# Seven block products in place of eight, in the experts' gate and up products and in the attention's output products of a two-layer block; one reordering of the up-projections' blocks

## The chip, the cores and the metric

The kernel runs on one core of a Trainium2 chip, as one program. The metric is the device time of one execution in microseconds. A "unit" below is one head of one batch row in the attention; a "tile" of the experts is one block of 128 gate columns and the 128 up columns that belong to it.

## The reference, cut to what matters

Two layers act on a residual stream of 4 x 512 rows of 512 values, all in float32. Layer 0 adds a test-time-training attention (a recurrence over 32 mini-batches of 16 tokens) and a gated feed-forward of 1408. Layer 1 adds a latent attention with 16 heads, here on sequences of 512, and four experts, each of which sees every fourth token. The change is in layer 1:

```python
xn = _layernorm(x)
# attention: latents c_kv (128) and c_q (384), 16 heads of 128, rotated first 64 dimensions
ctx = jnp.einsum('bhqk,bkhd->bqhd', softmax(q @ k / sqrt(D)), v).reshape(b, s, H * D)
attn = ctx @ W_O + b_O
# experts: token g*4 + e goes to expert e
gu = jnp.einsum('bgeh,ehd->bged', x4, gate_up_proj)
gate, up = (gu[..., :I], gu[..., I:])
inter = jax.nn.silu(gate) * up                     # I = 512
out = jnp.einsum('bgei,eih->bgeh', inter, down_proj)
x = x + attn + out.reshape(B, N, H)
```

## The kernel before, in words

The kernel has three stages, one after the other, with tile pools of their own.

**Layer 0** (0 to 967 us). The recurrence over mini-batches and the rest of the layer share the engines: `fill()` takes pieces of the feed-forward, of the projections and of the finishing of chunks from a generator (`between`, `take`) into the gaps of the recurrence. The stage goes through 8 chunks of 256 rows. In each, `gate_up` (L447 on) makes 11 blocks of the feed-forward: it loads `wg` and `wu` by SP's DMA queue (L454), multiplies 128x128 weights into 256 columns and puts both results into the two halves of one PSUM bank, `pf`; ACT applies Silu to the gate half (L458), VectorE multiplies (L459). `kv<-rows` (L290) and `z`, `zb` (L437, L439) are trips through DRAM on which the recurrence and the finishing of a chunk wait; `latents` writes the latents of layer 1 to DRAM (`lat_d`).

**Experts** (967 to 1145 us). `hidden(e)` makes, for each of 4 blocks of 128 gate columns, eight matmuls of 512 tokens: four into bank `pg` over the 512 input values and four into `pu` (`product`, L916 to L920). ACT applies Silu to `pg` (L946) and VectorE multiplies by `pu` into `inter` (L947). `returned(e)` multiplies `inter` by the down weights and adds into `y` (L961, L968). Two buffers of each bank are in turn. Beside them, `fold` prepares the weights of the first four heads of the attention.

**`fold`** (L821 on) is run once for each quarter of the heads. Of five matrices (`W_UK`, three blocks of `W_UQ`, `W_UV`) it loads four 128x128 blocks each (`raw`), as 16 DMAs of 16 KB in runs of 128 bytes (L856), so that VectorE's transposition within 32x32 squares (L846) gives the whole transpose. Matmuls then fold the rotation's weights (`pw`, L841) and the output weights (`pvo`, L865) in; `vo` holds, for each of 4 heads, 128 latent values by 512 outputs.

**Attention** (1145 to 2069 us). There are 64 units, 4 heads in each of 16 groups (4 quarters of the heads by 4 batch rows). Iteration i of the loop issues, in this order: queries and keys of unit i (`pk` L1047, `pq` L1055, rotations on VectorE and POOL L1030 to L1040), scores and softmax of unit i - 1 (`sc` L1065, maximum L1067, exponential L1070, scaling L1075, VectorE's transposition in squares L1094, then 16 DMAs that turn the blocks, `prT<-tt` L1125), one quarter of the output of a finished group (`po` L1146, added into `y` by VectorE at L1155), and the context of unit i - 3 (`pc` L1133, copied to `ctxT` by ACT at L1135). From the second step of a unit on, a step of `fold` follows. In the last two iterations two quarters of an output are made. `pin` keeps this order on PE, ACT and VectorE; POOL and the DMA queues are ordered by the scheduler. `pk`, `pq`, `po`, `pc`, `pw` and `pvo` take the four banks of one pool in turn, the scores another four. The last group's output is made in parts, as its heads become ready, with the last head's probabilities turned by PE.

The queries' latents `cq` of all four batch rows lie in SBUF throughout the attention, loaded once.

Of the kernel before, what the change touches and what calls it, by code (L numbers as in the profile page):

```python
# [12 lines left out]
F32 = mybir.dt.float32  # L13
# [5 lines left out]
P = 128  # L19
# [36 lines left out]
def trunk_kernel(ctx: ExitStack, tc: tile.TileContext, a: dict, out: bass.AP):  # L56
# [16 lines left out]
    lat_d = dram.tile([1 + QC // P, P, B, NCHUNK, CT], F32, tag="lat_d", name="lat_d")  # L73
    bo = const.tile([P, HS], F32, tag="bo", name="bo")
    eps_ttt = const.tile([P, 1], F32, tag="eps_ttt", name="eps_ttt")
    nc.vector.memset(eps_ttt, TTT_EPS)
# [12 lines left out]
    with ExitStack() as px:  # L89
# [9 lines left out]
        def mm(out, lhsT, rhs, start=True, stop=True):  # L99
            nc.tensor.matmul(out, lhsT=lhsT, rhs=rhs, start=start, stop=stop, skip_group_check=True)  # L100
# [347 lines left out]
        def gate_up(ch, i):  # L448
            if i == 0:
                hid[ch] = wk.tile([P, NI, CW], F32, tag="hid", name=f"hid_{ch}", bufs=1)  # L450
            pf = ps_ff.tile([P, 2, CW], F32, tag="pf", name=f"pf_{ch}_{i}")
            for j, nm in enumerate(("wg", "wu")):
                w = wk.tile([P, NC, P], F32, tag=nm, name=f"{nm}_{ch}_{i}")
                nc.sync.dma_start(out=w, in_=a[nm][i])  # L454
                for c in range(NC):
                    mm(pf[:, j, :], w[:, c, :], xTs[ch][:, c, :], c == 0, c == NC - 1)
            sg = wk.tile([P, CW], F32, tag="sg", name=f"sg_{ch}_{i}")
            nc.scalar.activation(sg, pf[:, 0, :], AF.Silu, scale=gs[:, i : i + 1])  # L458
            nc.vector.scalar_tensor_tensor(  # L459
                hid[ch][:, i, :], pf[:, 1, :], us[:, i : i + 1], sg, ALU.mult, ALU.mult  # L460
            )
            yield 3.43
# [330 lines left out]
    ckv = lat.tile([P, B, L], F32, tag="ckv", name="ckv")  # L793
    cq = lat.tile([P, QC // P, B, L], F32, tag="cq", name="cq")

# [18 lines left out]
    ups = ["uk"] + [f"uq{i}" for i in range(QC // P)]  # L814

    def group_tiles(pool, hg):
        w = {nm: pool.tile([P, HPG, D], F32, tag=nm, name=f"{nm}_{hg}", bufs=1) for nm in ups}
        w["vo"] = pool.tile([P, HPG, HS], F32, tag="vo", name=f"vo_{hg}", bufs=1)
        return w

    def fold(w, hg, wk, psum, bufs, pin=lambda ins: ins, ahead=1, rows=nc.sync):  # L821

        c = slice(hg * HPG * D, (hg + 1) * HPG * D)
        srcs = [a["W_UK"][:, c]] + [a["W_UQ"][i * P : (i + 1) * P, c] for i in range(QC // P)]
        for nm, src in zip(ups, srcs):
            nc.sync.dma_start(out=w[nm][:, :, :RD], in_=src.rearrange("p (h d) -> p h d", h=HPG)[:, :, :RD])
        srcs.append(a["W_UV"][:, c])
        raws, turned, ows = {}, {}, {}
# [4 lines left out]

        n = len(srcs)
        for i in range(n + 1 + ahead):
            k = i - ahead - 1
            if 0 <= k < n - 1:
                wt, wr, to = turned.pop(k), wqr if k else wkr, w[ups[k]]
                pw = psum(f"pw_{hg}_{i}").rearrange("p (h d) -> p h d", h=HPG)[:, :, :RD]
                for h in range(HPG):  # L840
                    pin(nc.tensor.matmul(pw[:, h, :], lhsT=wt[:, h, :], rhs=wr, start=True, stop=True))  # L841
                pin(nc.scalar.copy(to[:, :, RD:], pw))
            if 0 <= i - ahead < n:
                t = turned[i - ahead] = wk.tile([P, HPG, P], F32, tag="wt", name=f"wt_{hg}_{i - ahead}", bufs=bufs)
                pin(
                    nc.vector.transpose(  # L846
                        out=t.rearrange("p h c -> p (h c)"), in_=raws.pop(i - ahead).rearrange("p h c -> p (h c)")
                    )
                )
            if i < n:  # L850

                raw = raws[i] = wk.tile([P, HPG, P], F32, tag="raw", name=f"raw_{hg}_{i}", bufs=bufs)
                view = srcs[i].rearrange("(cq r) (h dq d) -> dq r h cq d", r=32, h=HPG, dq=4)
                for dq, r in enumerate(quarters):
                    for h in range(HPG):
                        nc.sync.dma_start(  # L856
                            out=raw[r, h].rearrange("r (cq d) -> r cq d", cq=4), in_=view[dq, :, h]
                        )
            if i - n - ahead + 1 >= 0:
                output_rows(i - n - ahead + 1)  # L860
            yield
# [19 lines left out]
    with ExitStack() as px:  # L881
# [33 lines left out]

        def product(e, ps, w, col):  # L916
            for c in range(NC):
                nc.tensor.matmul(  # L918
                    ps, lhsT=w[:, c, col : col + P], rhs=xe[:, :, c, e, :], start=(c == 0), stop=(c == NC - 1)
                )  # L920

        def by_chunk(ap):

            return ap.rearrange("p (k b j) -> p k b j", k=NCHUNK, b=B)

# [8 lines left out]
        def hidden(e):  # L934

            gu = ws.pop(e)
            inter = inters[e] = wk.tile([P, EI // P, B * P], F32, tag="inter", name=f"inter_{e}")
            for i in range(EI // P):
                if e > 1:
                    next(first, None)  # L940
                pg = ps_gu.tile([P, B * P], F32, tag="pg", name=f"epg_{e}_{i}")
                product(e, pg, gu, i * P)
                pu = ps_gu.tile([P, B * P], F32, tag="pu", name=f"epu_{e}_{i}")
                product(e, pu, gu, EI + i * P)
                sg = wk.tile([P, B * P], F32, tag="sg", name=f"esg_{e}_{i}")
                nc.scalar.activation(sg, pg, AF.Silu)  # L946
                nc.vector.tensor_mul(  # L947
                    by_batch(inter[:, i].rearrange("p (b j) -> p b j", b=B)), by_chunk(pu), by_chunk(sg)
                )
            if e + 2 < E:  # L950
                ws[e + 2] = gates(e + 2)

        def returned(e):
# [4 lines left out]
            for b in range(B):  # L958
# [9 lines left out]
                nc.vector.tensor_add(y[b][:, e, :], po, y[b][:, e, :])  # L968

        for e in range(E):  # L970
            if e == 1:
                nc.sync.dma_start(out=wqr, in_=a["W_QR"])
                nc.sync.dma_start(out=wkr, in_=a["W_KR"])
                buv16 = wk.tile([H, D], F32, tag="buv16", name="buv16", bufs=1)
                nc.sync.dma_start(out=buv16, in_=a["b_UV"].rearrange("(h d) -> h d", d=D))
                w0 = group_tiles(lat, 0)
                first = fold(w0, 0, wk, lambda nm: psp.tile([P, 512], F32, tag="pa", name=nm), 1)
                nc.sync.dma_start(out=buk, in_=a["b_UK"])
# [6 lines left out]
                nc.sync.dma_start(out=ckv, in_=lat_d[0].rearrange("p b k x -> p b (k x)"))  # L985
                for i in range(QC // P):
                    nc.sync.dma_start(out=cq[:, i], in_=lat_d[1 + i].rearrange("p b k x -> p b (k x)"))
            hidden(e)
# [27 lines left out]
    with ExitStack() as px:  # L1016
        wk = px.enter_context(tc.tile_pool(name="e_wk", bufs=2, reuse_waits="tile"))
        ps_pj = px.enter_context(tc.tile_pool(name="e_pspj", bufs=4, space=PSUM))
        ps_sc = px.enter_context(tc.tile_pool(name="e_pssc", bufs=4, space=PSUM))
# [22 lines left out]
        def queries_keys(hg, b, h, w):  # L1042
# [10 lines left out]
            for i in range(nq):  # L1053
                pin(
                    nc.tensor.matmul(  # L1055
                        pq, lhsT=w[f"uq{i}"][:, h, :], rhs=cq[:, i, b, :], start=(i == 0), stop=(i == nq - 1)
                    )
                )
# [71 lines left out]
        def context(prT, b, ctxT, h, nm, pool=ps_pj, tag="pj"):  # L1130
# [8 lines left out]
            )  # L1139

        def project_out(hg, b, e, w, ctxT, heads, po):
            if heads[0] == 0:
                po[e] = ps_pj.tile([P, HS], F32, tag="pj", name=f"po_{hg}_{b}_{e}")
            for h in heads:
# [18 lines left out]
        ws, cs, qk, probs = {}, {}, {}, {}  # L1163
        folds, outs = iter(()), []
        ws[0] = w0
        for i in range(nu + 1):
            if i < nu:
                hg, b, h = units[i]
                if h == 0:
                    if b == 1 and hg + 1 < NHG:  # L1170
# [10 lines left out]
                        )  # L1181
                        next(folds)
                    cs[hg, b] = wk.tile([P, HPG, L], F32, tag="ctxT", name=f"ctxT_{hg}_{b}")
                qk[i] = queries_keys(hg, b, h, ws[hg])
# [4 lines left out]
            for _ in range(1 if i < nu - 1 else 2):  # L1189
                if outs:  # L1190
                    outs.pop(0)()
            if i >= 3:
                hg, b, h = units[i - 3]
                context(probs.pop(i - 3), b, cs[hg, b], h, f"{i - 3}")
                if h == HPG - 1:
                    outs += [
                        (lambda hg=hg, b=b, e=e: project_out(hg, b, e, ws[hg], cs[hg, b], range(HPG), {}))
                        for e in range(E)
                    ]
            if i % HPG != 0:  # L1200
# [115 lines left out]
```

## Time and profile before

| what | value |
|---|---|
| runs | median 2072.76 us of 3 (2068.73 to 2076.26) |
| the profiled execution | 2071.4 us, of which the span from the first to the last instruction is 2069.5 |
| granted TensorE clock | 0.994 |
| `epg` and `epu` matmuls (L918) | 256 instructions, 58.4 and 57.5 us busy |
| `po` matmuls (L1146) | 512 instructions, 230.0 us busy |
| DMAs `raw` (L856) | 320 of 16 KB |
| DMA engines | mean 124 GB/s; q1 43.0% of 16 engines' span |

A row of the groups reads: line, engine, operation, result<-operands by the program's names, shape, count, busy time, mean time of one, and the idle time of the engine before it with what ended it. In the chain and the timeline the first number is the start in us from the span's beginning, the second the length, "x16" the number of instructions merged; in brackets stands the idle time before. SPq is the queue in which SP issues DMAs. A line of the waits gives who waited for whom, the total, how often, and the longest.

### The profile page before, as it was taken

How to read it: one execution, taken by the hardware profiler on the slowest of the kernel's cores; microseconds unless marked ns; L12 is line 12 of the kernel's file. 1: busy time of each engine (PE TensorE's matmuls, PEld its weight loads, DVE VectorE, ACT ScalarE, POOL GpSimd, SP SyncE). 2: the span in 40 equal slices, each digit the busy share in tenths (PEclk: the TensorE clock that was granted, in tenths of full speed). 3: DMA queues.
4: the chain of work that ended last, by engine and by line, in shares of the span. 5: the costliest groups of instructions: out<-in, count | busy, mean ns of one | idle time of the engine just before them, and what ended most of it. 6: DMA issues, size and time to landing. Idle time of an engine off the chain costs nothing.

```text
span 2069.5 us, 29404 instructions
## 1 busy us (share of the span) xinstructions
PE 2008.5 (97%) x9934; PEld 1144.4 (55%) x9934; DVE 1206.6 (58%) x2518; ACT 846.8 (41%) x1701; POOL 494.6 (24%) x559
## 2 busy tenths in 40 slices
PE   8999999899999999999999899999999999999999
PEld 6777676757676767645444344444444444444444
DVE  5446666474747575743121676666666666666662
ACT  2334343333434434312001464555555554555552
POOL 5233333233332323320000211121111111242110
PEclk9999999999999999999999999999999999999999
DMA  6546463545454747564721233443333333423332
GB/s 192 158 135 199 119 203 105 179 138 169 136 167 115 202 140 198 160 217 156 250 61 48 62 87 80 100 96 77 77 91 98 83 78 80 100 70 77 96 96 74
DMA packets 335730, 257.20 MB, mean 124 GB/s; under 512 B 107100, under 2 KB 264989, under 8 KB 334557
## 3 DMA queue, kind: packets, MB, share of 16 engines
q1 hardware_dynamic: 320592, 240.74, 43.0%
q0 software_dynamic: 3488, 9.27, 1.3%
q10 hardware_dynamic: 11500, 5.32, 0.9%
q8 instruction: 80, 1.31, 0.3%
q14 instruction: 70, 0.57, 0.1%
HBM read 159.50 MB, written 29.62 MB: 91 GB/s over the span
## 4 chain that ended last, share of the span: by engine, by line
PE 86%; DVE 7%; DMA 3%; ACT 2%; SPq 2%; issue 1%; POOL 0%; ACTq 0%; DVEq 0%; POOLq 0%
PE pj L100 13%; PE pf L100 12%; PE pc L1133 10%; PE po L1146 10%; PE sc L1065 10%; PE pq L1055 7%; PE pd L100 6%; PE epg L918 3%; PE epo L961 3%; PE epu L918 3%; PE pk L1047 3%; PE pz L100 2%; PE pso L100 1%; SPq L1125 1%; PE wacc L100 1%
## 5 line engine op out<-in xcount | busy, mean ns | idle before, releaser
L1070 ACT ACTIVATE prob<-sc,mx 128x512 f32<-128x512 f32 x256 | 174.5, 684 | 173.6 <-DVE mx L1067 169.6
L1133 PE MATMUL pc<-prT,lv 128*128 128x512 f32 x496 | 226.3, 599 | 8.8 <-issue 4.1
L1065 PE MATMUL sc<-kT,qT 96*128 96x512 f32 x512 | 230.9, 593 | 1.8 <-ACT prob L1070 1.5
L1146 PE MATMUL po<-vo,ctxT 128*128 128x512 f32 x512 | 230.0, 592 | 0.7 <-ACT ctxT L1135 0.7
L1040 POOL TENSOR_TENSOR kT<-t_k,t_k 32x512 f32<-32x512 f32 x64 | 80.7, 1261 | 562.4 <-PE pq L1055 454.8
L1094 DVE STREAM_TRANSPOSE tt<-prob 128x512 f32<-128x512 f32 x252 | 172.8, 705 | 71.5 <-ACT prob L1075 45.1
L100 PE MATMUL pf<-xT,wg 128*128 128x256 f32 x704 | 174.2, 390 | 13.1 <-DVE hid L459 6.8
L1075 ACT ACTIVATE prob<-prob,sm 128x512 f32<-128x512 f32 x256 | 176.5, 714 | 0.0
L1055 PE MATMUL pq<-cq,uq 128*128 128x512 f32 x384 | 175.2, 592 | 0.0
L1067 DVE TENSOR_REDUCE mx<-sc 128x1 f32<-128x512 f32 x256 | 168.3, 678 | 5.8 <-PE sc L1065 3.8
L100 PE MATMUL pf<-xT,wu 128*128 128x256 f32 x704 | 167.7, 381 | 0.0
L1133 PEld LDWEIGHTS pc<-prT,lv 128*128 128x128 f32 x496 | 94.8, 192 | 131.0 <-issue 125.0
L1065 PEld LDWEIGHTS sc<-kT,qT 96*128 96x128 f32 x512 | 96.7, 190 | 125.8 <-issue 120.3
L100 PE MATMUL pd<-wd,hid 128*128 128x512 f32 x352 | 165.6, 600 | 0.6 <-DMA wd<-in_wd 0.5
L1146 PEld LDWEIGHTS po<-vo,ctxT 128*128 128x128 f32 x512 | 96.9, 190 | 123.4 <-issue 118.2
L100 PEld LDWEIGHTS pf<-xT,wg 128*128 128x128 f32 x704 | 132.9, 193 | 40.7 <-DVE hid L459 8.6
L100 PEld LDWEIGHTS pf<-xT,wu 128*128 128x128 f32 x704 | 134.4, 191 | 18.9 <-DMA wu<-in_wu 0.3
L1055 PEld LDWEIGHTS pq<-cq,uq 128*128 128x128 f32 x384 | 73.0, 190 | 91.8 <-issue 90.2
L459 DVE SCALAR_TENSOR_TENSOR hid<-pf,us,sg 128x256 f32<-128x256 f32 x88 | 41.7, 475 | 134.7 <-ACT sg L458 133.7
L1030 DVE SCALAR_TENSOR_TENSOR t_k<-pk,b_UK,trig_k 32x512 f32<-32x512 f32 x64 | 47.9, 748 | 113.0 <-ACT kT L1048 110.9
L297 POOL TENSOR_SCALAR sk<-k,m 128x256 f32<-128x256 f32 x64 | 61.3, 971 | 192.1 <-PE pz L100 172.6
L404 POOL TENSOR_SCALAR gh<-grad,m 128x256 f32<-128x256 f32 x64 | 62.6, 988 | 153.8 <-DVE grad L373 146.2
(251 smaller groups left out, 2994.7 us busy)
## 6 DMA issues: line engine op xcount, KB each, us to landing
prT<-tt SPq DMA_DIRECT2D x1008, 64.0 KB, 2.0
wd<-in_wd SPq DMA_DIRECT2D x176, 256.0 KB, 3.0
wg<-in_wg SPq DMA_DIRECT2D x88, 256.0 KB, 2.8
wu<-in_wu SPq DMA_DIRECT2D x88, 256.0 KB, 3.4
rows<-rows SPq DMA_DIRECT2D x128, 66.0 KB, 2.2
kv<-rows SPq DMA_DIRECT2D x32, 264.0 KB, 4.9
gu<-in_gu SPq DMA_DIRECT2D x3, 2048.0 KB, 7.8
xt<-in_x SPq DMA_DIRECT2D x32, 128.0 KB, 2.9
```

What stands on the lines that cost most here:

```text
L100: nc.tensor.matmul(out, lhsT=lhsT, rhs=rhs, start=start, stop=stop, skip_group_check=True)
L404: nc.gpsimd.tensor_scalar_mul(gh[:, :, h, :], g, m2[:, h : h + 1])
L918: nc.tensor.matmul(ps, lhsT=w[:, c, col : col + P], rhs=xe[:, :, c, e, :], start=(c == 0), stop=(c == NC - 1))
L1040: nc.gpsimd.tensor_sub(t[RD:mid, :], t1[RD:mid, :], t2[RD:mid, :])
L1055: nc.tensor.matmul(pq, lhsT=w[f"uq{i}"][:, h, :], rhs=cq[:, i, b, :], start=(i == 0), stop=(i == nq - 1))
L1065: pin(nc.tensor.matmul(ps, lhsT=qT[:KQ, i * P : (i + 1) * P], rhs=kT[:KQ, :], start=True, stop=True))
L1067: pin(nc.vector.tensor_reduce(mx, ps, AX.X, ALU.max, negate=True))
L1070: pin(nc.scalar.activation(pr, ps, AF.Exp, bias=mx, scale=1.0, accum_out=sm))
L1075: pin(nc.scalar.mul(pr, pr, sm))
L1094: nc.vector.transpose(out=tt[:, :, :, i, :], in_=pr.rearrange("p (kb e j) -> p kb e j", e=2, j=K))
L1133: pin(nc.tensor.matmul(pc, lhsT=lv[:, b, k, :], rhs=prT[:, k, :], start=(k == 0), stop=(k == E - 1)))
L1146: nc.tensor.matmul(po[e], lhsT=ctxT[:, h, e * P : (e + 1) * P], rhs=w["vo"][:, h, :], start=(h == 0), stop=(h == HPG - 1),)
```

## The change

Both places now multiply a 2 x 2 arrangement of blocks by seven block products and fifteen sums (Winograd's form of Strassen's method), with the sums of the right-hand operand made once. The sum that is needed three times is built up in one half of a PSUM bank (`x`), and read out after each of its steps.

- *Experts.* Of a tile, rows of the left matrix are gate and up columns, its columns the two halves of the 512 input values; the right matrix is the tokens, in two halves of 256. `left_sums` (VectorE, four sums of 128x256, one of them in place in the weights) is issued one tile ahead; `right_sums` (four sums of 128x512) once for an expert. A block product is two matmuls of 256 columns. ACT copies `x` and `pu` out four times a tile (`c1`, `c2`, `c3`, `c5`, one buffer each); VectorE makes three additions and two multiplies in place of one multiply.
- *Attention.* Four heads' contexts of a group (a 512 x 512 matrix) by `vo`. The generator `outputs` makes one block product in its first step and two in each of three more, a step to a unit; a block product is four matmuls of 256 columns. POOL makes the sums (`left_operands` for a group, `right_operands` for a quarter of the heads). VectorE adds each result into `y` where it belongs: 8 additions of 128x512 for a group in place of 4. The last group keeps `project_out`. One of the projections' four banks becomes the bank of `x`.
- *Reordering once.* 80 DMAs copy the up-projections' blocks from DRAM to DRAM during layer 0 (`blocks_d`, one after each of the first ten blocks of `gate_up` in each chunk), 64 KB each in runs of 128 bytes; `fold` then loads four blocks with one DMA in place of 16.
- *Room in SBUF.* The queries' latents are loaded for each group (three DMAs of 256 KB, one group ahead, two buffers), and `wt` in `fold` has one buffer. One of the two latent buffers serves the experts for the four copies.

The diff, cut to its core:

```diff
+    blocks_d = dram.tile([QC // P + 2, P, H, P], F32, tag="blocks_d", name="blocks_d")
+    up_srcs = [a["W_UK"]] + [a["W_UQ"][i * P : (i + 1) * P] for i in range(QC // P)] + [a["W_UV"]]
+    def reordered():
+        for k, src in enumerate(up_srcs):
+            view = src.rearrange("(cq r) (h dq d) -> cq dq r h d", r=32, dq=4, d=32)
+            for cq in range(4):
+                for dq in range(4):
+                    nc.sync.dma_start(
+                        out=blocks_d[k, 32 * dq : 32 * dq + 32, :, 32 * cq : 32 * cq + 32], in_=view[cq, dq]
+                    )
+                    yield
...
+            if i < 10:
+                next(copies, None)
...
-    cq = lat.tile([P, QC // P, B, L], F32, tag="cq", name="cq")
+    s_ops = lat.tile([P, 3, 2, L // 2], F32, tag="s_ops", name="s_ops")
+    t_ops = lat.tile([P, 4, 2, HS // 2], F32, tag="t_ops", name="t_ops")
...
-                view = srcs[i].rearrange("(cq r) (h dq d) -> dq r h cq d", r=32, h=HPG, dq=4)
-                for dq, r in enumerate(quarters):
-                    for h in range(HPG):
-                        nc.sync.dma_start(
-                            out=raw[r, h].rearrange("r (cq d) -> r cq d", cq=4), in_=view[dq, :, h]
-                        )
+                nc.sync.dma_start(out=raw, in_=blocks_d[i][:, heads, :])
...
+        def left_sums(gu, i):
+            s1, s2, s4 = (s_ops[:, n, :, i % 2 * P : (i % 2 + 1) * P] for n in range(3))
+            nc.vector.tensor_add(s1, a21, a22)
+            nc.vector.tensor_sub(s2, s1, a11)
+            nc.vector.tensor_sub(a21, a11, a21)
+            nc.vector.tensor_sub(s4, a12, s2)
...
-                product(e, pg, gu, i * P)
-                product(e, pu, gu, EI + i * P)
-                sg = wk.tile([P, B * P], F32, tag="sg", name=f"esg_{e}_{i}")
-                nc.scalar.activation(sg, pg, AF.Silu)
+                pg = ps_gu.tile([P, 2, half], F32, tag="pg", name=f"epg_{e}_{i}")
+                pu = ps_gu.tile([P, half], F32, tag="pu", name=f"epu_{e}_{i}")
+                x = pg[:, 0]
+                block_product(x, o["a11"], tokens(e, 0, 0), True)
+                block_product(pg[:, 1], o["a12"], tokens(e, 1, 0))
+                nc.scalar.copy(c1, x)
+                block_product(x, o["s2"], t_ops[:, 1])
+                nc.scalar.copy(c2, x)
+                block_product(pu, o["s1"], t_ops[:, 0], True)
+                nc.scalar.copy(c5, pu)
+                block_product(x, o["s3"], t_ops[:, 2])
+                nc.scalar.copy(c3, x)
+                block_product(pu, o["s4"], tokens(e, 1, 1))
+                block_product(x, o["a22"], t_ops[:, 3])
+                g = wk.tile([P, 2, half], F32, tag="sg", name=f"esg_{e}_{i}")
+                nc.vector.tensor_add(g[:, 0], pg[:, 1], c1)
+                nc.vector.tensor_add(g[:, 1], pu, c2)
+                nc.scalar.activation(g, g, AF.Silu)
+                nc.vector.tensor_add(c5, c5, c3)
+                for h, up in enumerate((x, c5)):
+                    nc.vector.tensor_mul(to[:, k], by_chunk(up), by_chunk(g[:, h]))
...
-        ps_pj = px.enter_context(tc.tile_pool(name="e_pspj", bufs=4, space=PSUM))
+        ps_pj = px.enter_context(tc.tile_pool(name="e_pspj", bufs=3, space=PSUM))
+        ps_x = px.enter_context(tc.tile_pool(name="e_psx", bufs=1, space=PSUM))
...
+        def block_product(ps, a, w, start=True):
+            for k in range(2):
+                for q in range(2):
+                    pin(nc.tensor.matmul(ps[:, q, :], lhsT=a[:, k, q * P : (q + 1) * P], rhs=w[:, k, :], ...))
...
+            x = bank(ps_x, "px", "px")
+            block_product(x, left_blocks(c)["a11"], r["b11"])
+            add(x, 0, 0)
+            o = left_operands(c)
+            yield
+            p2 = bank(ps_pj, "pj", "p2")
+            block_product(p2, o["a12"], r["b21"])
+            block_product(x, o["s2"], r["t2"], False)
+            add(p2, 0, 0)
+            add(x, 0, 1)
+            yield
+            p5 = bank(ps_pj, "pj", "p5")
+            block_product(p5, o["s1"], r["t1"])
+            block_product(x, o["s3"], r["t3"], False)
+            add(p5, 0, 1)
+            add(p5, 1, 1)
+            add(x, 1, 1)
+            yield
+            p3 = bank(ps_pj, "pj", "p3")
+            block_product(p3, o["s4"], r["b22"])
+            block_product(x, o["a22"], r["t4"], False)
+            add(p3, 0, 1)
+            add(x, 1, 0)
...
             for _ in range(1 if i < nu - 1 else 2):
-                if outs:
-                    outs.pop(0)()
+                next(outs, None)
```

`add` is a pinned `tensor_add` on VectorE into a quarter of `y[b]`; `left_operands` and `right_operands` are four `nc.gpsimd` additions or subtractions each, by the same scheme as `left_sums` and `right_sums`.

## The prediction

> **What bounds the kernel now.** I read the busy times first, then the chain that ended last, then the waits and the timeline of each stage.
>
> ```profile
> span 2069.5 us, 29404 instructions
> PE 2008.5 (97%) x9934; PEld 1144.4 (55%) x9934; DVE 1206.6 (58%) x2518; ACT 846.8 (41%) x1701; POOL 494.6 (24%) x559
> PE 86%; DVE 7%; DMA 3%; ACT 2%; SPq 2%; issue 1%; POOL 0%; ACTq 0%; DVEq 0%; POOLq 0%
> ```
>
> TensorE is busy for 97% of the span and is 86% of the chain: time goes only if matmul time goes. By stages PE is busy 922.1 of 967.0 us (layer 0), 177.8 of 178.0 (967 to 1145, experts) and 908.6 of 924.5 (attention). So both places of the change are bound by PE, and the question is what half-width products cost. Two pieces of the chain:
>
> ```profile
> 506.40 3.65 PE pf L100 x16
> 516.03 3.45 PE pf L100 x16
> ...
> 1185.70 3.44 PE sc L1065 x8
> ```
>
> Sixteen instructions of 256 columns take 3.45 us undisturbed (215.6 ns each), eight of 512 columns 3.44 (430 ns). Each f32 matmul is two instructions, and every one has its own weight load (190 ns), which fits under 215 ns. So half-width products run at full rate, and seven in place of eight save an eighth. (The means of 390 and 592 ns in the groups are latencies.)
>
> **The experts' gate and up products.** For each of 16 tiles, 8 matmuls of 512 columns (16 instructions x 0.430 = 6.88 us) become 14 of 256 (28 x 0.2156 = 6.04): 0.84 saved, 13.5 us in all. What can give it back is the hand-over, since one half bank accumulates three running sums, each copied by ACT before PE goes on.
>
> ```profile
> 828.63 1.89 PE L100 MATMUL pf<-xT,wu 128*128 128x256 f32 x8
> ...
> 830.55 0.47 ACT L458 ACTIVATE sg<-pf,gs 128x256 f32<-128x256 f32 x1 [3.73 <-PE pf L100]
> ```
>
> The gate half was written before 828.63, yet its Silu starts at 830.55, 0.2 us after the last matmul into the other half (issued until 830.35): a reader waits for the whole bank. The rule behind it is in the Trainium skill, "PSUM — Partial Sum Buffer", section "PSUM bank collisions raise a hardware error": two engines must not touch one bank at once. It speaks against packing x and the second half into one bank; without it the loop below would be some 0.9 us shorter and cost nothing, by it 4 us.
>
> ```profile
> 1455.77 0.37 ACT L842 COPY uk<-pw 128x256 f32<-128x256 f32 x1 [0.25 <-PE pw L841]
> ```
>
> - The copy of a sum: 0.2 until ACT starts, 0.37 for a 128x256 copy, 0.05 back, together 0.62. The cover is one block product (0.86) less the prefetched weight load (0.215): 0.645. It just fits: I take 0; if the cover goes, 0.2 a hand-over.
> - The closed loop of a tile: c5 is one buffer, so its next copy waits for the last multiply. From the end of a tile's last product: 0.2, add 0.42 (L523, 128x256), hand-over 0.05, Silu 0.60 (L946), 0.05, two multiplies 2 x 0.42, 0.05, copy 0.37, 0.05 = 2.6; then four block products, 3.45, and a weight load of 0.19 not hidden: 6.25 against 6.04. Cost 0.25 x 16 = 4 us. Bounds: 0 (where `pw`, `pvo` or `epo` matmuls stand between) and 0.8 a tile (all four hand-overs late), 13.
> - VectorE: per tile 4 left sums, 3 adds and 2 multiplies of 256 elements, 9 x 0.42 = 3.8 of 6.0 us, and four sums of 512 an expert (4 x 0.69). It was nearly idle (30.6 busy of 178), so this is hidden, except at the start: VectorE ends layer 0's last latent at 971.0, the PE at 970.0. In the changed program 8 left sums (3.4) and t1 (0.7) follow, so s1·t1 can start at 975.1; PE has four block products ready (3.45) and waits from 973.4 on: 1.7 to 1.9 us. The table load before the first Silu (1.28) pushes the second tile's copies: 1.1.
>
> Sum for the experts: -13.5 + 4 + 1.9 + 1.1 = **-6.5 us** (bounds -13.5 and +1).
>
> **The attention's output products.** For 15 of 16 groups of four heads, 32 instructions x 0.430 = 13.76 become 56 x 0.2156 = 12.07: 1.69 x 15 = 25.3 us. The last group keeps the old form. Here the running sum is handed over a whole unit (one head, 13.7 us) later, so the adds are off the path, but the pool for projections has 3 banks in place of 4. One unit as it is:
>
> ```profile
> 1459.06 3.60 PE L1065 MATMUL sc<-kT,qT 96*128 96x512 f32 x8
> ...
> 1462.50 3.60 PE L1146 MATMUL po<-vo,ctxT 128*128 128x512 f32 x8
> ...
> 1465.93 3.60 PE L1133 MATMUL pc<-prT,lv 128*128 128x512 f32 x8
> ...
> 1468.48 0.65 DVE L1155 TENSOR_TENSOR y<-po,y 128x512 f32<-128x512 f32 x1
> ...
> 1470.22 2.74 PE L1055 MATMUL pq<-cq,uq 128*128 128x512 f32 x6
> ```
>
> VectorE adds an output 9.4 us after the scores begin, behind the four transposes of the softmax, as its order is fixed. `pq` of the next unit now takes the bank of this output (three back in the rotation): released at 10.07, or at 10.72 in the step with two adds of p5; its weights load at 10.74. It just fits: 0 to 0.1 us a group, 0.5 in all; if VectorE fell behind by 1 us, 1 us in 45 units. Four more adds a group (4 x 0.65) fall where VectorE waits 2.1 us for ACT anyway. POOL gets 4 sums a group (L1205: 1.27 each, 5.1 us), 4 more once for each quarter of the heads; it idles 9.9 us a unit, and rotations pushed back 5 us are needed 10 us later: 0.
>
> The end is the exception: in the last units two steps of group 15 run in one unit. x·t2 waits for the add of the first sum, 10.07 after the scores' start, while PE arrives at 3.44 + 1.72 + 1.72 = 6.88: a stall of 3.2 us (from 0, were the add ahead of the transposes, to 4.3, if the unit after also stalls).
>
> The fold's 16 small loads a step become one.
>
> ```profile
> 1706.10 7.67 SPq L856 DMA_DIRECT2D raw<-in_W_UQ  x16
> 1713.88 20.88 SPq L1125 DMA_DIRECT2D prT<-tt  x32
> ...
> 1725.99 3.67 PE L1133 MATMUL pc<-prT,lv 128*128 128x512 f32 x8 [2.71 <-issue]
> ...
> PE pc L1133 <- issue: 4.1, 3, 2.7
> PE pc L1133 <- DMA prT<-tt: 1.5, 2, 1.2
> ```
>
> SP's queue spends 7.7 us on them, the turned probabilities leave late, and `pc` waits: 5.6 us in five places. Latents by group add 3 loads per four units (about 1.3 us of SP). I take 4.5 of the 5.6 as gone (bounds 0 and 5.6). What is late next is nothing that these waits show.
>
> Sum for the attention: -25.3 + 0.5 + 3.2 - 4.5 = **-26 us** (bounds -31 and -15).
>
> **Layer 0, where the blocks are copied.** 80 copies of 64 KB, 512 pieces of 128 bytes each. On SP: `z<-zch`, also 512 pieces, takes 0.54 to issue; 80 x 0.54 = 43 us, in a queue that waits 241 us for `pf` and 141 for `pd`. On the DMA engines: 1246.5 to 1255, mostly such pieces, moved 2390 packets with a share of 25.2%, or 14 ns each; the mean over q1 is 44. So 0.5 to 1.4 us a copy, 4 to 12 points on a share of 55%. The Trainium skill, "DMA: Bandwidth & Descriptors", section "Specifications", calls 512 bytes the least for line rate, below it a read-modify-write; were the copies to cost twice, an estimate of 80 to 230 us of DMA time would result, which still fits beside the loads. No row shows a copy from DRAM to DRAM. On PE's path lie the boundaries of chunks, where `kv` landing (4.9 us) ends the chain; one copy ahead of it at each of 8 boundaries costs 0 to 1.4 each. The changed program also orders layer 0's work anew, and of its 45 us of idle PE time some may fill or open. I take **+2**, bounds -4 and +12.
>
> **Sum.** -6.5 - 26 + 2 = -30.5 on the profiled execution's 2071.4 (span 2069.5 and 1.9 around it): 2040.9. The median of the runs, 2072.8, is 1.4 above that execution, inside their spread of 7.5; I say **2041**.
>
> **Rivals.**
> - *All of it arrives* (0.13): nothing lost in the experts but the start, all 5.6 us of waits gone, layer 0 unchanged: 2071.4 - 13.5 + 3 - 27.7 = 2033, down to 2028 if layer 0 fills. For it: the hand-overs fit on paper.
> - *ACT's hand-over becomes the experts' bound* (0.13): 0.8 a tile, so their gain is gone (+0.5): 2047; with layer 0 at +8, 2053. For it: 0.645 against 0.62 leaves nothing.
> - *The change doesn't do what it says* (0.05): half-width products come at the disturbed 3.65 per sixteen; 28 x 0.228 = 6.39 and 56 x 0.228 = 12.77 save 7.8 + 14.9 in place of 38.8: 2057. Against: undisturbed rows are 3.45.
> - *Slower* (0.05): the copies stand before `kv<-rows` in SP's queue and rings, and the serial steps of layer 0 wait for it. 1.4 us at each of 32 steps is 45 us: 2071.4 - 32.5 + 45 = 2084. It decides from 1.02 us a step on. Against: 31.0 us of waits for `kv` come from 8 occasions only, elsewhere it is early.
>
> **How the numbers follow.** The forecast gets 0.62; 0.02 is left for no change. Range 2028 to 2057: the two cases above and below it are taken in; left out are slower and the edges. Within 0.3% (6 us), about what a measurement of this kernel can tell from no change, only a mixture of rivals falls: 0.02. Faster 0.93, slower 0.05.
>
> **What will show it.** PE busy about 39 us less, near 1970, with 16 instructions of 256 columns at 3.45 us in `epg` and `po`'s successors; experts 171 us in place of 178, with short waits of PE on ACT copies and VectorE; four-unit period in the attention 53.2 us in place of 54.9; no waits of `pc` on issue; a wait of about 3 us for VectorE near the end; layer 0 within 963 to 979. I am wrong if PE's waits in the attention grow by 1 us a unit, or if layer 0 is longer by more than 12 us.

## The result, and the profile after

The changed kernel takes 2068.5 us (median of 17 runs) beside 2075.6 for the kernel before on the same chip: ratio 0.9966, interval 0.9955 to 0.9977. That is 7 us less; 31 were forecast, and the range (2028 to 2057) doesn't hold it. The profiled execution has a span of 2067.1 (before: 2069.5).

The page of the changed kernel, the lines that answer to those shown before:

```profile
span 2067.1 us, 30725 instructions
...
PE 1983.4 (96%) x10486; PEld 1255.6 (61%) x10486; DVE 1302.3 (63%) x2722; ACT 866.2 (42%) x1763; POOL 587.5 (28%) x635
...
PE 46%; SPq 2%; DVE 2%; ACT 1%; DMA 1%; issue 0%; DVEq 0%; ACTq 0%
```

The chain (third line) is followed back to 997 us only, where a latent of VectorE waits for a store, so its shares make 52% and say nothing of layer 0. TensorE's busy time fell by 25.1 us, but the span by 2.4 only: the rest became idle time. (The medians differ by 7.1: the profiled execution of the kernel before is 4.2 shorter than its median, that of the changed kernel 0.3 longer.) Cut at the first matmul of the experts (`epg`) and of the attention (`pk`), the span says where:

| us | before | changed | difference | forecast |
|---|---|---|---|---|
| layer 0, to the end of its last matmul | 969.9 | 981.2 | +11.3 | +2 |
| wait for the tokens | 0 | 7.0 | +7.0 | not seen |
| experts | 175.7 | 180.5 | +4.8 | -6.5 |
| attention | 923.9 | 898.5 | -25.4 | -26 |

The attention does what was forecast, and everything in front of it loses it again. The row of layer 0 is the least certain: its 969.9 is the shortest of the eight executions below that have the same order of TensorE's instructions there, which go up to 978.6. First the attention, in a unit of the changed kernel (start, length, work of TensorE):

```profile
1486.04 3.60 PE L1134 MATMUL sc<-kT,qT 96*128 96x512 f32 x8
1489.47 1.89 PE L1245 MATMUL p<-t_ops,s_ops 128*128 128x256 f32 x8
1491.20 1.89 PE L1245 MATMUL px<-t_ops,ctxT 128*128 128x256 f32 x8
1492.93 3.60 PE L1202 MATMUL pc<-prT,lv 128*128 128x512 f32 x8
```

Eight half-width instructions begin every 1.73 us (216 ns each) with nothing idle between. The two block products take the 3.44 that eight full-width ones took, and the step with one block product (at 1518.77) takes 1.73: 1.7 us saved every fourth unit.

Now the border of layer 0 and the experts. GpSimd's queue in the changed kernel (in brackets the idle time before, and who ended it):

```profile
904.88 1.27 POOL L496 TENSOR_TENSOR yf<-yf,xr 128x512 f32<-128x512 f32 x1
968.20 0.20 POOL L833 MEMSET ones<- 128x128 f32 x1 [62.05 <-PE pj L144]
968.92 0.83 POOL L924 DMA_DIRECT2D gu<-in_gu  x1 [0.52 <-ACT lat L644]
969.76 3.73 POOL L928 DMA_DIRECT2D xe<-xe_d  x7
```

The same queue in the kernel before:

```profile
894.77 0.20 POOL L813 MEMSET ones<- 128x128 f32 x1
894.92 0.83 POOL L906 DMA_DIRECT2D gu<-in_gu  x1
907.69 4.26 POOL L910 DMA_DIRECT2D xe<-xe_d  x8 [11.93 <-DMA z<-zch]
```

A tile of ones, which is needed only near the end of the attention, is filled 0.2 us before the first expert's weights and tokens are loaded. It now waits 62 us, and the loads behind it start 74 and 62 us later. The addresses in the built programs give the reason: the new tiles made the pool `lat` 2 KB larger in each partition and moved `ones` from byte 99712 (over `yf` of chunk 6, long done) to 89472, over `x1` of the last chunk, which the last transpositions of layer 0 (L144) read. What TensorE makes of it, behind a line of the kernel before, in which it waits for nothing there:

```profile
969.94 3.60 PE L918 MATMUL epg<-xe,gu 128*128 128x512 f32 x8
```

```profile
973.91 7.28 PE L117 MATMUL pj<-xl,W_DQ 128*128 128x256 f32 x32
988.15 5.29 PE L966 MATMUL epg<-xe,gu 128*128 128x256 f32 x16 [6.96 <-DMA xe<-xe_d]
1000.82 2.93 PE L966 MATMUL epu<-t_ops,s_ops 128*128 128x256 f32 x6 [7.38 <-DVE t_ops L947]
```

7.0 us without tokens; then four block products, and 7.4 us without the first right sum. VectorE was itself late with it: two of its last four latents waited 9.3 us each for a buffer, until its store to DRAM (`lat_d`) had landed, while the loads of the experts, all at once now, filled the DMA engines (share 1.02 from 990 to 1010). Its last latent ended at 997.3. The transposition that is the subject of e1 costs TensorE 2.3 us here.

In layer 0 most of the 11 us come before 200 us. TensorE in the changed kernel:

```profile
169.92 3.70 PE L117 MATMUL pd<-wd,hid 128*128 128x512 f32 x8
179.54 0.44 PE L117 MATMUL pso<-a_bd,gh 128*32 128x68 f32 x2 [5.92 <-POOL gh L421]
179.77 0.42 PE L117 MATMUL wacc<-g_bd,km 128*32 128x64 f32 x2
180.12 3.78 PE L117 MATMUL pf<-xT,wu 128*128 128x256 f32 x8
```

In the built program one matmul of `pso` and one of `wacc` of mini-batch 4 stand 40 to 50 places further forward than before, ahead of four matmuls of `pf` that were ready; the queue stands behind them until GpSimd has made `gh`. From the third update of the state (`wacc`) to the fourth it is 39.8 us in place of 29.9. The order differs in other places of layer 0 too, also ahead of the third update.

### The profile page after: what moved, and what is told of

Its sections match the earlier page's. It is cut to its first block, busy times and chain, and to the rows that moved or that the text cites. A ratio compares the mean times of both kernels' runs of the same rounds, so it can differ in the third digit from the quotient of the medians.

```text
span 2067.1 us, 30725 instructions
## 1 busy us (share of the span) xinstructions
PE 1983.4 (96%) x10486; PEld 1255.6 (61%) x10486; DVE 1302.3 (63%) x2722; ACT 866.2 (42%) x1763; POOL 587.5 (28%) x635
## 4 chain that ended last, share of the span: by engine, by line
PE 46%; SPq 2%; DVE 2%; ACT 1%; DMA 1%; issue 0%; DVEq 0%; ACTq 0%
PE pc L1202 9%; PE sc L1134 9%; PE pq L1124 7%; PE px L1245 5%; PE p L1245 4%; PE epg L966 3%; PE epo L1029 3%; PE pk L1116 2%; SPq L1194 2%; PE epu L966 1%; PE po L1302 1%; PE pw L865 1%; PE pvo L883 1%; ACT prob L1139 1%; DVE tt L1163 0%
## 5 line engine op out<-in xcount | busy, mean ns | idle before, releaser
L1139 ACT ACTIVATE prob<-sc,mx 128x512 f32<-128x512 f32 x256 | 174.3, 683 | 157.6 <-DVE mx L1136 152.7
L117 PE MATMUL pf<-xT,wg 128*128 128x256 f32 x704 | 175.7, 392 | 12.5 <-DVE hid L478 6.8
L1144 ACT ACTIVATE prob<-prob,sm 128x512 f32<-128x512 f32 x256 | 176.3, 713 | 0.0
L117 PEld LDWEIGHTS pd<-wd,hid 128*128 128x128 f32 x352 | 63.6, 190 | 58.7 <-issue 44.6
L477 ACT ACTIVATE sg<-pf,gs 128x256 f32<-128x256 f32 x88 | 41.5, 473 | 135.1 <-PE pf L117 134.7
L1109 POOL TENSOR_TENSOR qT<-t_q,t_q 32x512 f32<-32x512 f32 x64 | 80.7, 1260 | 56.9 <-DVE t_q L1105 56.8
```

What stands on the lines that cost most here:

```text
L1109: nc.gpsimd.tensor_sub(t[RD:mid, :], t1[RD:mid, :], t2[RD:mid, :])
L1139: pin(nc.scalar.activation(pr, ps, AF.Exp, bias=mx, scale=1.0, accum_out=sm))
L1144: pin(nc.scalar.mul(pr, pr, sm))
```

## Experiments

One table holds all of them, from the profiled execution of each (the attention to the span's end), with the median and the ratio to the kernel before on the same chip. "Update" is the time from the third to the fourth update of the state; layer 0 ends with its last matmul. Layer 0 as a whole is the least certain column. The third update comes at 158.4 to 165.1 in the eight executions with TensorE's order of before, also where no instruction ahead of it differs (158.4 before, 165.1 in e2), and at 155.6 to 157.6 in the six with the changed order (changed, e1, e3, e5, e9, e11); the end of layer 0 at 969.9 to 978.6 and at 978.5 to 981.2. So the changed order loses some 9 us in the fourth update, but had gained a few ahead of the third.

| run | update | layer 0 | token wait | experts | attention | median | ratio, interval |
|---|---|---|---|---|---|---|---|
| before | 29.9 | 969.9 | 0 | 175.7 | 923.9 | | 1 |
| changed | 39.8 | 981.2 | 7.0 | 180.5 | 898.5 | 2068.5 | 0.9966 (0.9955 to 0.9977) |
| e1 ones late | 38.1 | 978.5 | 0 | 180.7 | 898.2 | 2058.7 | 0.9934 (0.9913 to 0.9956) |
| e2 ones on late tile | 30.2 | 978.4 | 15.1 | 178.3 | 923.8 | 2089.5 | 1.0086 (1.0057 to 1.0115) |
| e3 copies alone | 38.5 | 979.4 | 0 | 176.3 | 922.0 | 2082.1 | 1.0042 (1.0025 to 1.0058) |
| e4 copies on GpSimd | 30.4 | 973.5 | 0 | 176.8 | 921.7 | 2075.9 | 1.0019 (1.0003 to 1.0035) |
| e5 transposes in place | 38.4 | 980.1 | 0 | 166.1 | 898.9 | 2046.9 | 0.9863 (0.9841 to 0.9885) |
| e6 all three | 30.8 | 973.0 | 0 | 165.9 | 898.4 | 2043.6 | 0.9847 (0.9824 to 0.9871) |
| e7 experts alone | 30.9 | 977.0 | 0 | 165.9 | 916.9 | 2060.9 | 0.9936 (0.9912 to 0.9961) |
| e8 attention alone | 31.0 | 974.5 | 0 | 175.6 | 898.6 | 2050.8 | 0.9883 (0.9861 to 0.9905) |
| e9 order alone | 38.9 | 979.6 | 0 | 177.1 | 925.0 | 2080.2 | 1.0030 (1.0013 to 1.0048) |
| e10 fold alone | 31.8 | 978.6 | 0 | 175.6 | 917.1 | 2070.1 | 0.9990 (0.9980 to 1.0001) |
| e11 transposes alone | 38.8 | 979.2 | 7.4 | 176.1 | 898.9 | 2062.9 | 0.9954 (0.9937 to 0.9970) |
| e12 ones left | 31.0 | 974.2 | 9.2 | 175.8 | 899.1 | 2055.4 | 0.9917 (0.9901 to 0.9934) |

**e1, the ones behind the loads.** The changed kernel with

```diff
-    nc.gpsimd.memset(ones, 1.0)
...
+        nc.gpsimd.memset(ones, 1.0)
         ws = {0: gu, 1: gates(1)}
```

> The changed kernel with one instruction moved: GpSimd's fill of the 64 KB tile of ones stands behind its token loads instead of ahead of the first expert's weight load. Theory A (placement): that fill lies in the grown pool on the last chunk's token tile, waits 62.0 us for its last transposes, and holds GpSimd's weight and token loads back by some 74 us; with it moved, the loads start near 895 us again, the 7.0 us wait for tokens and the 7.4 us wait for the first right sum go, and most of the slow-clock stretch behind them: 14 to 20 us less than the changed kernel (2068.5), so 2049 to 2055. Theory B (the tiles of the weights and tokens themselves now lie on late tiles of layer 0, or the loads collide with the block copies): the loads start no earlier than about 960 us and the time stays within 3 us of 2068.5.

Theory A holds for the loads: weights at 903.56, tokens from 916.60, no wait for tokens, 0.96 for the right sum. But only 9.7 us of span were gained, 6.6 by the ratios, and 2058.7 lies above the band. The experts are as long as before the edit, because another wait has opened, in VectorE and, through ScalarE's copy, in TensorE:

```profile
999.79 0.43 DVE L1011 TENSOR_TENSOR hold<-hold 128x256 f32<-128x256 f32 x1 [0.50 <-ACT hold L1004]
1012.87 0.71 DVE L869 STREAM_TRANSPOSE wt<-raw 128x512 f32<-128x512 f32 x1 [12.64 <-DMA raw<-blocks_d]
1013.50 0.39 DVE L1008 TENSOR_TENSOR esg<-epg,hold 128x256 f32<-128x256 f32 x1
```

```profile
1001.72 1.03 PE L966 MATMUL epu<-t_ops,s_ops 128*128 128x256 f32 x4
1014.86 2.07 PE L966 MATMUL epg<-t_ops,s_ops 128*128 128x256 f32 x4 [12.11 <-ACT hold L998]
```

The fold's first transposition stands in VectorE's queue ahead of a sum of the first expert's third tile (L1008) and of all that follows, and its raw block isn't there. Silu waits for VectorE's sum, the copy of the next `x` stands behind Silu in ScalarE's queue, and TensorE may not add to `x` before it is copied. In the kernel before the same transposition waited longer and cost TensorE nothing:

```profile
1019.98 0.71 DVE L846 STREAM_TRANSPOSE wt<-raw 128x512 f32<-128x512 f32 x1 [14.75 <-DMA ow<-in_W_O]
```

**e2, the ones on the late tile.** The kernel before, with one declaration moved:

```diff
+    ones = lat.tile([P, P], F32, tag="ones", name="ones")
     lv = lat.tile([P, B, E, KVC], F32, tag="lv", name="lv")
...
-    ones = lat.tile([P, P], F32, tag="ones", name="ones")
```

> The kernel before, with the declaration of the tile of ones moved ahead of another tile of its pool, so that it lies at the address on which it lies in the changed kernel. No arithmetic, load or copy differs. Theory A (placement alone): GpSimd's fill waits until about 960 us here too, weights and tokens of the first expert come some 60 us later, and the kernel is 7 to 16 us slower than before (2083 to 2092). Theory B (the loss at the border belongs to the block products and their sums on VectorE): within 3 us of before.

1.0086, about 18 us slower: theory A, a little above its 7 to 16. In the built program `ones` lies at 89408 here, 64 bytes from its place in the changed kernel and over the same `x1`. The fill waited 62.0 us, the weights' load was issued at 965.98, and TensorE stood 15.1:

```profile
965.26 0.21 POOL L813 MEMSET ones<- 128x128 f32 x1 [61.99 <-PE pj L127]
```

```profile
971.32 7.07 PE L100 MATMUL pj<-xl,W_DQ 128*128 128x256 f32 x32
993.53 6.21 PE L918 MATMUL epg<-xe,gu 128*128 128x512 f32 x8 [15.14 <-DMA xe<-xe_d]
```

So the loss at the border needs no block product: where one 64 KB tile lies is enough. (The profiled execution, 2097.4, is the longest of four, the others 2087.3 to 2090.2; its layer 0 is 8.5 longer than before, of which 6.7 come ahead of the third update. Token wait and experts together, 17.7, are the loss by the runs.)

**e3, e4 and e9, the copies.** The kernel before with the 80 copies of the change and no reader; in e4 from another queue; in e9 with one row of 32:

```diff
-                    nc.sync.dma_start(
+                    nc.gpsimd.dma_start(
...
-out=blocks_d[k, 32 * dq : 32 * dq + 32, :, 32 * cq : 32 * cq + 32], in_=view[cq, dq]
+out=blocks_d[k, 32 * dq : 32 * dq + 1, :, 32 * cq : 32 * cq + 32], in_=view[cq, dq, :1]
```

> The kernel before with the 80 block copies of layer 0 added and nothing reading them. Theory C (the copies change the order in which TensorE's instructions are scheduled: one matmul of the state update's output, pso, is put some 40 places early and the queue stands behind it for 5.9 us, with about 3 us of slower clock after it): 8 to 11 us slower than before (2084 to 2087), with that wait near 180 us. Theory D (the copies cost nothing here, and the changed kernel's 10 us in layer 0 come from its other tiles): within 2 us of before.

> The kernel before with the same 80 copies, issued from GpSimd's queue instead of SyncE's; TensorE's order in layer 0 is then the one of before. Theory C (order): the wait of 5.9 us is not there, and the time is within 3 us of before. Theory E (traffic: 10 MB more through memory in layer 0 slow the weights' loads): 8 to 11 us slower, as with the copies on SyncE's queue. If GpSimd's own issue of the copies delays its small products, a wait of TensorE for gh or km shows at other places, 2 to 15 us.

> The kernel before with the 80 copies on SyncE's queue cut to one row of 32 each (a 32nd of their bytes; nothing reads them). TensorE's order is the one with the copies. Theory C (order): the 5.9 us wait for gh near 180 us is there, and the kernel is 5 to 9 us slower than before, as with the whole copies (8.7 by medians). Theory E (traffic, or the queue's time for large copies): within 3 us of before.

e3 is 8.7 us slower (0.42%), e9 6.2 (0.30%), with intervals that overlap; both have TensorE's order of the changed kernel, an update that is 8.6 and 9.1 us longer, and this line (here of e9):

```profile
PE pso L115 <- POOL gh L419: 5.9, 1, 5.9
```

In e4 TensorE's order is that of before, the line is gone, the update is 0.5 longer, and 3.9 us (0.6 to 7.3) are lost. So the order makes the longer update, not the 10 MB: with a 32nd of the bytes it is as long. What the order costs in the end is less than the update shows, since the same order brings the third update forward: 6.2 us by e9, 4.8 by e3 less e4, each a difference with several us of doubt. What e4 still loses isn't settled: on GpSimd's queue the copies are issued early (between 25 and 170 us; between 14 and 457 on SyncE's queue in the changed kernel), and that early part varies by itself. Theory E stands for at most those few us. e3 against e9 shows no price of the copies' 128-byte pieces that can be told from zero. The page "DMA: Bandwidth & Descriptors" of the Trainium skill, section "Specifications", calls 512 bytes the least for line rate, with a read-modify-write below it; a price of it isn't seen here, and at most e4's 3.9 us leave room for one.

**e5 and e6, the second and third repair.** e5 is e1 with the transposes of `fold` kept at their place (the first then stands 36 rows later in VectorE's order); e6 is e5 with e4's edit:

```diff
-                pin(
+                tc.keep_in_program_order(
                     nc.vector.transpose(
```

> The changed kernel with the tile of ones filled behind the token loads, and with the fold's five VectorE transposes in the experts kept at their place in the program. Theory F (with the block products VectorE's queue is part of TensorE's chain: the first transpose, placed ahead of the second expert's sums, waited 12.6 us for its raw block, which had cost the kernel before nothing, and TensorE lost 12.1 us there and some 3 us to a slower clock): the wait goes, 11 to 15 us less than with the ones alone moved (2058.7), so 2044 to 2048. Rival G (the wait is only moved: the raw block or the loads ahead of it hold up the next user, or the hand-over by ScalarE's copies is what bounds the first experts): less than 4 us gained, 2055 to 2059.

> As the run before, and the 80 block copies issued from GpSimd's queue, which gives layer 0 TensorE's order of before. Theory C (order): the wait of 5.9 us near 180 us goes, 4 to 8 us less than with the first two edits: 2037 to 2043, and in all 32 to 38 us less than the kernel before, which would be about the forecast of 2041. If copies on GpSimd's queue cost more than SyncE's order did (second loads or small products of GpSimd late at the end of layer 0): no gain, 2044 to 2050.

e5: 0.9863 after 0.9934, 14.7 us by the ratios and 12.3 by the spans, all of it in the experts (180.7 to 166.1): theory F. e6 gains 7.8 more by the spans, nearly all of it in the update, but only 3.3 by the ratios, whose intervals overlap, so that 2043.6 lies just above the band: its profiled execution (2039.2) is the shortest of four, the others 2043.0 to 2046.6. That layer 0's order is worth anything is therefore not shown by this pair of runs alone. At 1.5% less than the kernel before, e6 has the lowest median here. What TensorE still waits for in its experts and attention:

```profile
PE px L1245 <- DVE y L1266: 3.2, 1, 3.2
PE pc L1202 <- DMA prT<-tt: 2.9, 1, 2.9
...
PE pbo L895 <- DVE bo_part L888: 1.2, 1, 1.2
PE epg L966 <- ACT hold L998: 1.0, 1, 1.0
PE epu L966 <- DVE t_ops L947: 1.0, 1, 1.0
```

**e7, e8 and e10, the parts by themselves.** All on the base of e6. In e7 and e10 the output products are the old ones; in e8 and e10 `hidden` is that of the kernel before, without left and right sums:

```diff
         def outputs(hg, b, w, c):
+            for e in range(E):
+                project_out(hg, b, e, w, c, range(HPG), {})
+                yield
```

> As the run before (ones behind the loads, transposes in place, copies on GpSimd's queue), but the attention's output products are the old ones, eight 512-wide products; only the experts' products are by seven blocks. The forecast's terms: experts 13.5 us less in TensorE work, 4 to 7 us given back to hand-overs, start and table load; copies 2 to 4 us: 1 to 10 us below the kernel before, 2064 to 2073. If the hand-over loop bounds the experts (ScalarE's four copies a tile): no gain, 2074 to 2080.

> The same base with the experts' products as before, and only the attention's output products by seven blocks. The forecast's terms: 25.3 us less TensorE work, 0.5 for the reused bank and 3.2 at the end given back, fold's stalls gone: 21 to 27 us, less 2 to 4 for the copies: 2049 to 2057. If what was seen as the attention's gain belongs to the fold's new loads alone: 2067 to 2074.

> No block products at all: experts and output products are the old ones; the copies (on GpSimd's queue), the fold's whole-block loads, the latents read again by batch, ones and transposes as in the run of all three. Theory H (the shorter loads of the fold take away stalls worth 7 us in the attention, as its length with the old output products says: 916.9 against 923.9): copies 2 to 4 us lost, 5 to 8 gained, 1 to 6 us below the kernel before, 2068 to 2073. Rival (those 7 us belong to something else than the fold's loads): 2 to 5 us above, 2076 to 2079.

On the base of e6 the sections are the same in whatever company they run: experts 165.9 with block products and 175.6 without (9.7 less), attention 898.5 with them and 917.0 without (18.5 less). 917.0 against 923.9 (6.9) comes with no block product: the fold's loads, with the other things that e7 and e10 keep, the latents by group and three banks in place of four. Of it 5.6 are the two waits of `pc` that the prediction named, which are both gone in e10. With the old fold the traces of e2, e3, e4 and e9 have 921.7 to 925.0, so 6.9 is 5 to 8. e7 came out below its band, since the closed loop, for which 4 us were allowed, costs almost nothing: a tile takes 6.09 where its matmuls alone take 6.04 (the same product of two tiles in e6):

```profile
996.30 1.03 PE L966 MATMUL epu<-t_ops,s_ops 128*128 128x256 f32 x4
...
1002.39 1.03 PE L966 MATMUL epu<-t_ops,s_ops 128*128 128x256 f32 x4
```

e8 lies in its band. e10's fold pays for its copies, and no gain is left that can be told from zero (0.9990).

**e11 and e12, which loss hides which.** e11 is the changed kernel with e5's edit alone, e12 is e6 without that of e1.

> The changed kernel with only the fold's transposes kept in place; ones and copies as in the change. Theory I (the losses hide behind each other: while the late loads hold the experts back, the first raw block is waited for only 2.8 us, TensorE stands 2.3 us): 2 to 6 us less than the changed kernel (2068.5), 2063 to 2067. If the losses simply add: 12 us less, as between the two runs with ones moved, 2055 to 2058.

> All three edits but the one on the tile of ones, which is filled ahead of the loads as in the change. Theory A and I: against the run of all three (2043.6) this shows the whole price of the late loads with nothing else to hide it, 15 to 21 us as in the kernel before with ones on the late tile (17.9): 2058 to 2065. If the price is only what moving it alone gave (10): 2052 to 2056.

e11: 0.9954 after 0.9966, 2.5 us by the ratios and not 12 (5.5 by the spans; the intervals of the ratios overlap). While the late loads hold the experts back, the raw block arrives nearly in time.

e12 decides less. Its median, 2055.4, lies in the band of the rival (2052 to 2056). Against e6 it is 14.5 us by the ratios, between the rival's 10 and the 15 of theory A and I, and 21.0 by the spans (token wait 9.2, experts 9.9 longer, layer 0 1.2), but its profiled execution is the longest of four (2060.2, the others 2052.9 to 2055.5).

That the two losses hide each other rests on four runs with the copies on SyncE's queue. By the ratios, moving the ones alone gives 6.6 us (e1), keeping the transpositions alone 2.5 (e11), and both 21.4 (e5), more than twice the sum. With the transpositions in place, moving the ones is worth 18.9 (e11 to e5), about what the tile's place costs in e2.

## Why the prediction was wrong, and where it was right

Its sum, -30.5, is what e6 shows (-31.7 by the ratio, -36.5 to -26.7), which is in part luck, as the experts gave 3 us more than their sum, and two errors of the attention's terms cancel. TensorE's savings were sound; three waits that the change brings along, of which the terms held next to nothing, took 25 us back (0.9966 against 0.9847).

- **Half-width products at full rate: right.** 216 ns each, beside each other and beside full-width ones. The rival with 3.65 us per sixteen is out.
- **The attention, -26: right, with other parts.** -25.4. The fold gave 6.9 (4.5 taken), the block products 18.5 (21.6 taken: -25.3 + 0.5 + 3.2). The stall of 3.2 us at the end is there to the tenth, `pbo` waits 1.2 for the same adds, and behind the stall the granted clock is 0.50 from 1990.0 to 1993.3 in e6, an estimated 1.7 us. The bank that was to "just fit" fits.
- **The experts, -6.5: the terms mis-sized, and in the changed kernel overrun.** With the border in order it is -9.7: the loop's 0.25 a tile (0.21 by the prediction's own 6.25 and 6.04) is 0.05, the wait at the start 1.0 in place of 1.9, the table load 1.0 in place of 1.1; about 1 us of the 3.8 given back is not accounted for. In the changed kernel it is +4.8.
- **"It was nearly idle [...], so this is hidden, except at the start", for which 1.7 to 1.9 us were taken: the step that failed.** The start was worked out with weights and tokens there by 970 and VectorE free at 971.0. In the changed kernel TensorE stood 7.0 us for tokens and 7.4 for the first right sum, and VectorE's last latent ended at 997.3. "Hidden" failed as well: VectorE's busy time wasn't the question. Once Silu and the copies of `x` hang on its sums, its queue is part of TensorE's chain, and whatever waits in that queue, waits for TensorE: 2.3 us in the changed kernel, 12.1 in e1, for a transposition whose longer wait had been free. The prediction asked what the change adds to VectorE, not what already stood there waiting.
- **The missing term behind it.** No step looked at the loads of the first expert, since the diff leaves them alone. They are queued behind a fill whose address the change moved: 18 us by e2, overlapping with the transposition.
- **Layer 0, +2 (-4 to +12): the mechanism named, the centre wrong.** "Orders layer 0's work anew" is what happened, and it took +11.3 between the two profiled executions, near the upper bound; by the runs the copies with the order cost the kernel before 8.7 (e3). The copies' own transfers, on which the step spent its numbers, are the smaller part, at most e4's 3.9. The slower rival (copies ahead of `kv`) isn't seen: the wait is for `gh`, in one place.

Of what was to show it: PE busy near 1970 was 1983.4 (part of it is the slower clock after the waits; e6 has 1975.0), the experts' 171 was 180.5, the four-unit period (53.3 from 1626.27 on), the absence of `pc` waits on issue and the 3 us near the end were as said, layer 0 was 2 us over its band. "Wrong if layer 0 is longer by more than 12 us" was nearly met; the point that decided, the border, was not on the list.

## What to carry to other kernels

A change that adds or resizes tiles moves other tiles; ask of every early load and fill near a border which tile it now lies on and who reads that last, and which instruction stands ahead of it in its queue. A hand-over that puts an idle engine into the critical engine's chain makes all the waits of that engine count: list them from the trace before. Compare the order of the critical engine's instructions before and after, also in stages that the change only brushes: here two matmuls put forward made one update of the state 9 us longer.

## What the runs showed of the hardware

A wait of TensorE can cost more than its length. After 7.0 us idle the 16 instructions at 988.15 took 5.3 us (3.6 at 978.45 in e1, where nothing was waited for), after 15.1 us the first eight full-width ones of e2 took 6.2 (3.6 in the kernel before), after 5.9 us the 16 half-width ones of `pf` from 180.12 on took 6.4 in place of 3.5: 1.7 to 2.9 us on top. The granted clock of the 20 us around was 0.78 (970 to 990), 0.78 (990 to 1010 in e2) and 0.85 (180 to 200). For the 5.9 us wait near 180 us, this makes 8.8 of the 9.9 by which the update grew.

The Trainium skill, "TensorE: Matmul & The Clock Gate", "Part 1: The HAM clock gate", says that an idle window of about 3.4 us halves the clock and another busy one restores it; an estimate from it is 1.7 us a stall, the least of the three above. The traces agree on the half: the granted clock was 0.50 from 984.6 to 991.3 and from 179.1 to 185.8. They don't agree on the idle time that it takes. In the changed kernel a wait of 2.3 us was enough: the granted clock was 0.50 from 1025.6 to 1028.9, and 12 half-width instructions took 4.4 us in place of 2.6.

```profile
1024.91 1.51 PE L966 MATMUL epg<-t_ops,s_ops 128*128 128x256 f32 x4 [2.29 <-ACT hold L998]
```
